# First attention of a two-layer decoder: where the maxima of the next heads stand, how the causal mask reaches them, and how the sums are grouped

## The chip, the cores and the metric

The kernel runs on one core of a Trainium2 chip. A core has TensorE (PE: matmuls, with PEld its weight loads), VectorE (DVE), ScalarE (ACT), GpSimd (POOL) and SyncE (SP, which here issues the DMAs). Each engine works through its own queue in order; semaphores make one wait for another. Matrix products land in PSUM, which has 8 banks of 128 partitions x 512 float32. The metric is the device time of one execution in microseconds, the median of the runs shown.

## What is computed

x is (4, 1024, 256) float32. Two layers follow each other, each with an attention, a cross attention to a context of 77 rows, and a feed-forward part:

```python
x = x + _L0_attn_ref(_layernorm(x), L0_attn_w_attn, L0_attn_w_proj)
x = x + _L0_xattn_ref(_layernorm(x), ctx_768, ...)
x = x + _L0_ffn_ref(_layernorm(x), ...)
x = x + _L1_attn_ref(_layernorm(x), L1_attn_W)
x = x + _L1_xattn_ref(_layernorm(x), ctx_768, ...)
x = x + _L1_ffn_ref(_layernorm(x), ...)
```

The change touches the first line alone, a causal attention of 16 heads of 16 columns with a bias that falls linearly with distance:

```python
q, k, v = jnp.split(x @ w_attn.T, 3, axis=-1)      # then (B, 16, 1024, 16)
att = jnp.einsum('bhqd,bhkd->bhqk', q, k) * (1.0 / math.sqrt(D))
rel = pos[None, :] - pos[:, None]
bias = jnp.where(rel <= 0, slopes * rel, -jnp.inf)
att = jax.nn.softmax(att + bias[None], axis=-1)
y = jnp.einsum('bhqk,bhkd->bhqd', att, v)
return y.transpose(0, 2, 1, 3).reshape(B, T, C) @ w_proj.T
```

## The kernel before

The first attention (A0) goes batch by batch, and in a batch by four groups of four heads. Queries and keys stand in two bfloat16 stacks per group, QS and KS, in which each value is split into several bfloat16 rows so that one matmul gives a nearly exact product; 12 further rows carry the bias, and two more rows of QS, against ones in KS, carry minus the row's maximum. So the maxima must be known before the scores are made.

**Maxima** (`a0_max`, L339). For a group, 38 units in all. Each unit fills a PSUM bank M with up to 512 columns of scores, query-major (L352), and DVE takes the maximum along the row (L357) into a small tile mt. There are 22 units whose last 128 columns lie on the diagonal: per half of the queries one with four heads side by side, two with two heads, and eight with one head and 384 or 512 columns. On these a further matmul adds the mask (L356: identity times a tile with -30000 above the diagonal). Sixteen units per group have no diagonal. Two PSUM banks serve M in turn. After each half, `a0_put_max` (L375) negates the maxima (L380), transposes them on PE (L381), splits them into two bfloat16 rows (L383, L384) and sends these by two small DMAs (L386) into rows 108 and 109 of QS.

**Units** (`a0_main`, L388). A unit is a chunk c of 256 queries and a block j of 128 keys up to the diagonal, 2 + 4 + 6 + 8 = 20 units per group. `scores` makes, key-major, S for two heads at a time in one of two banks (L401), adds the transposed mask on diagonal blocks (L403), and ACT takes the exponential into the tile P (L404), which has four buffers. `pv` makes the **sums** (L413): for each of the four heads V's 17 columns (16 of values, one of ones), padded to 32, times P, in float32, which PE runs as two passes. The four heads stand in four column tiles of 32, so eight instructions of PE make the sums of one unit. A unit's sums are issued two units later (`LAG0` = 2): whenever more than two are pending, the oldest is done. The list of pending ones is kept from one group to the next. When a chunk pair is through, `o_out` (L424) moves O out, transposes it (L430) and divides by the sum column.

**Order.** `A0` (L470) weaves a group's 20 units with the front work of the next group: its stacks (seven DMAs or so) and its 38 maxima. In the third group the first 12 steps of the next batch's front (layernorm, q, k and v) are woven in too, and in the fourth group the rest of that front, 44 steps with the first group's maxima of the next batch. `weave(a, na, b, nb)` takes the next step of whichever is behind in proportion, so that na steps of a go with nb steps of b; what is left of the one runs alone when the other is through. The weights of b are the row `NW`, 20 being that of a. Around all this a second weave adds the cross attention and feed-forward of the preceding batch, or, in the first batch, the preparation of weights. The program's order is not yet that of the queues: the build asks the framework to order every engine's queue by a simulated timeline (`schedule_with_timeline_sim=True`), so an instruction can come before others that stand ahead of it in the program, as far as data and buffers allow.

The second attention (A1, L923 to L927 for its sums) has the same form of sums, with 8, 16 or more instructions in a row. Its tile DL0 is allocated once, when it starts.

## Time and profile before

| what | value |
|---|---|
| median of 3 runs | 2410.97 us (2407.53 to 2416.93) |
| profiled execution | 2408.58 us |
| its span | 2406.8 us |
| PE busy | 2141.5 us, 89% |
| DVE busy | 1692.2 us, 70% |
| ACT busy | 1639.2 us, 68% |
| POOL busy | 1198.2 us, 50% |
| mean granted PE clock | 0.957 |
| maxima on DVE, L357 | 608 instructions, 386.2 us, mean 655 ns |
| maxima on PE, L352 | 768 instructions, 225.8 us busy |
| scores, L401 | 1280 instructions, 230.4 us busy |
| sums, L413 | 2560 instructions, 240.1 us busy |
| exponentials, L404 | 640 instructions, 342.4 us, mean 563 ns |

The span runs from the first to the last instruction of the program; the profiled execution's own time lies 1.8 us above it. Busy time counts an instant once even where several instructions of an engine overlap, as matmuls do: a matmul's duration runs from its start to the end of its way through the array, and the next one starts long before. So the distance from one start to the next says what a matmul costs in a full queue.

In the lists that follow, a waits row names the waiting engine and line, then who released it, the sum of the waiting in us, how often, and the longest. A row of the timeline gives start, duration, engine and line, and tiles, with equal neighbours merged (x2), and in brackets the idle time ahead of it with its releaser. A row by shape gives the count, busy us and mean ns, then the engine's idle time ahead and who ended it. A windows row gives, for a stretch of the span, each engine's busy time and count of instructions.

### The profile page before, as it was taken

What the parts mean: (1) busy time and instruction counts of PE and PEld (TensorE: products, weight loads), DVE (VectorE), ACT (ScalarE), POOL (GpSimd) and SP (SyncE); (2) the same over time, 40 slices, a digit from 0 to 9 for tenths busy, and PEclk for the clock granted to TensorE, in tenths of its full rate; (3) what the DMA queues carried; (4) which work ended last, traced back from release to release, by engine and by line L of the source; (5) the groups of instructions that cost most, each with busy time, mean ns of one, the idle gap of its engine ahead of it and who ended that gap; (6) DMA issues with size and microseconds to landing.
All of it is one profiled execution on the core that took longest, in us unless ns stands there. A gap on an engine that the chain in (4) does not pass through costs nothing.

```text
span 2406.8 us, 51445 instructions
## 1 busy us (share of the span) xinstructions
PE 2141.5 (89%) x19110; PEld 1510.9 (63%) x19110; DVE 1692.2 (70%) x3781; ACT 1639.2 (68%) x4173; POOL 1198.2 (50%) x1942
## 2 busy tenths in 40 slices
PE   6798899998999998899988988889988998899876
PEld 4454457755666654576656766567766766676675
DVE  4666657677766786776775677777867787777766
ACT  4365446676766676565778878987678777888542
POOL 7121313154331352412545458766867788775664
PEclk9899999999999999899989999999989999999988
DMA  8667331223841236231262224512241223542000
GB/s 260 199 193 211 116 90 44 66 61 108 242 135 44 64 111 188 69 73 41 81 185 53 71 71 129 149 38 56 98 111 43 56 74 119 105 98 71 10 10 18
DMA packets 182697, 238.45 MB, mean 99 GB/s; under 512 B 16198, under 2 KB 165846, under 8 KB 175958
## 3 DMA queue, kind: packets, MB, share of 16 engines
q1 hardware_dynamic: 182446, 235.15, 34.8%
q8 instruction: 151, 2.47, 0.4%
q14 instruction: 100, 0.82, 0.1%
HBM read 152.62 MB, written 82.21 MB: 98 GB/s over the span
## 4 chain that ended last, share of the span: by engine, by line
PE 59%; DVE 14%; DMA 8%; POOL 7%; ACT 7%; issue 3%; SPq 1%; POOLq 0%; DVEq 0%; ACTq 0%
PE T L191 10%; PE W L191 8%; PE O L413 7%; PE O L927 5%; PE S L401 5%; PE Q L191 4%; PE M L352 4%; PE S L898 3%; DVE P L904 2%; DVE s_mt L357 2%; PE W L630 1%; PE T L723 1%; DMA wst<-in_L_xattn_Wq 1%; POOL P L909 1%; ACT P L906 1%
## 5 line engine op out<-in xcount | busy, mean ns | idle before, releaser
L357 DVE TENSOR_REDUCE s_mt<-M 128x1 f32<-128x512 f32 (+3 forms) x608 | 386.2, 655 | 137.9 <-PE M L356 100.0
L404 ACT ACTIVATE P<-S 128x512 f32<-128x512 f32 (+1 forms) x640 | 342.4, 563 | 154.7 <-PE S L401 78.5
L906 ACT ACTIVATE P<-P,eps 128x1024 f32<-128x1024 f32 x320 | 344.5, 1082 | 57.2 <-DVE P L904 52.6
L904 DVE TENSOR_REDUCE P<-S 128x512 f32<-128x512 f32 (+1 forms) x480 | 284.8, 610 | 75.4 <-PE S L898 60.7
L352 PE MATMUL M<-KS,QS 108*128 108x512 bf16 (+3 forms) x768 | 225.8, 341 | 48.2 <-DVE s_mt L357 23.9
L191 PE MATMUL T<-R,xX 128*128 128x352 f32 (+1 forms) x1136 | 246.7, 331 | 4.8 <-ACT E L619 1.4
L898 PE MATMUL S<-QS,KS 96*128 96x256 bf16 (+1 forms) x1280 | 217.9, 269 | 36.9 <-DVE P L904 34.5
L401 PE MATMUL S<-QS,KS 110*128 110x256 bf16 (+1 forms) x1280 | 230.4, 267 | 16.9 <-ACT P L404 13.7
L413 PE MATMUL O<-P,V 128*32 128x256 f32 (+1 forms) x2560 | 240.1, 377 | 0.8 <-ACT P L404 0.6
L622 POOL TENSOR_TENSOR E<-E,s_xsm 128x616 f32<-128x616 f32 x64 | 77.9, 1217 | 323.7 <-DVE s_xsm L620 261.3
L191 PEld LDWEIGHTS T<-R,xX 128*128 128x128 f32 x1136 | 183.0, 190 | 24.7 <-ACT E L619 5.4
L191 PE MATMUL W<-R,xph 128*128 128x256 f32 (+1 forms) x952 | 185.4, 292 | 6.5 <-DVE xpl L180 4.8
L909 POOL TENSOR_TENSOR P<-P,y 128x512 f32<-128x512 f32 x128 | 165.1, 1299 | 34.0 <-ACT y L871 17.4
L619 ACT ACTIVATE E<-T,s_xmx 128x77 f32<-128x77 f32 x512 | 159.6, 334 | 28.6 <-DVE s_xmx L616 26.5
L401 PEld LDWEIGHTS <-KS 110*128 110x128 bf16 x1280 | 107.2, 100 | 105.6 <-issue 60.3
L927 PE MATMUL O<-P,VsJ 128*32 128x128 f32 x3584 | 168.2, 282 | 5.3 <-ACT P L906 4.8
L898 PEld LDWEIGHTS <-KS 96*128 96x128 bf16 x1280 | 101.8, 99 | 110.2 <-issue 88.9
L191 PEld LDWEIGHTS W<-R,xph 128*128 128x128 f32 (+1 forms) x952 | 149.5, 192 | 17.8 <-DVE xpl L180 6.9
L352 PEld LDWEIGHTS <-QS 108*128 108x128 bf16 x768 | 68.3, 100 | 128.0 <-issue 100.4
L191 PE MATMUL W<-R,xpl 128*128 128x256 f32 (+2 forms) x476 | 139.6, 293 | 1.0 <-DVE xpl L180 1.0
L730 POOL TENSOR_TENSOR R<-wst 128x256 f32<-128x256 f32 x128 | 92.3, 732 | 88.0 <-DVE wst L729 82.8
L179 ACT ACTIVATE xph<-W 128x512 fp32r<-128x512 f32 (+2 forms) x180 | 79.3, 458 | 80.1 <-PE W L633 32.8
(351 smaller groups left out, 5660.0 us busy)
## 6 DMA issues: line engine op xcount, KB each, us to landing
QS<-dr SPq DMA_DIRECT2D x144, 192.0 KB
KS<-dr SPq DMA_DIRECT2D x72, 384.0 KB
dr<-qp SPq DMA_DIRECT2D x32, 768.0 KB
MD<-R SPq DMA_DIRECT2D x24, 616.0 KB
UD<-R SPq DMA_DIRECT2D x24, 512.0 KB
R<-MD SPq DMA_DIRECT2D x32, 308.0 KB
X<-in_x SPq DMA_DIRECT2D x16, 512.0 KB
dr<-qp SPq DMA_DIRECT2D x32, 256.0 KB
```

The lines of the kernel that those rows point to most:

```text
L191: nc.tensor.matmul(out, x, y, start=first and n == 0, stop=last and n == len(seq) - 1)
L352: nc.tensor.matmul(Sv[:, x, 0:w], QS[:108, i // 4, hh, i % 4 * 128 : i % 4 * 128 + 128], KS[:108, hh, k0:k1], start=x == 0, stop=not diag ...
L357: nc.vector.tensor_reduce(out, Sv[:, :, 0:w], AX.X, ALU.max)
L401: nc.tensor.matmul(S[:, e, 0:w], st[1][:110, hh, j * 128 : (j + 1) * 128], st[0][:110, q0 // 512, hh, q0 % 512 : q0 % 512 + w], start=e == ...
L404: nc.scalar.activation(P[:, 2 * p : 2 * p + 2, 256 - w :], S[:, :, 0:w], AF.Exp)
L413: nc.tensor.matmul(O[0][hh * 32 : hh * 32 + 32, o + o0 : o + 256], V[j // 4][:, j % 4, h * 17 : h * 17 + 32], P[:, hh, o0:], start=c % 2 = ...
L619: nc.scalar.activation(E[:, n * 77 : (n + 1) * 77], Sv[:, k, :], AF.Exp, bias=mx[:, n : n + 1], accum_out=sm[:, n : n + 1])
L898: nc.tensor.matmul(S[:, e, 0:w], st[r][1][:96, hh, j * 128 : (j + 1) * 128], st[r][0][:96, q0 // 512, hh, q0 % 512 : q0 % 512 + w], start= ...
L904: nc.vector.tensor_reduce(Pv, S[:, :, 0:w].unsqueeze(3), AX.X, ALU.max, apply_absolute_value=True)
L906: nc.scalar.activation(Pw, Pw, AF.Square, bias=self.eps1)
L909: nc.gpsimd.tensor_tensor(Pd, Pd, Ds[r, c][:, j - 2 * c], ALU.mult)
L927: nc.tensor.matmul(Oc[rows, o0 : o0 + 128], lhs, P[:, hh, c0 : c0 + 128], start=j == 2 * c and i == 2 * c, stop=fin and i == 2 * c + 1)
```

## The change

Three edits to the first attention.

1. The weave weights of the front work go from 25, 25, 38, 38 per 20 units to 42, 42, 54, 48.
2. On diagonals of one head, the mask matmul goes. DVE adds a mask tile of 512 columns (zeros, and the triangle in its last 128; the last w columns of it are used) and takes the maximum in one `tensor_tensor_reduce`, which also writes the masked scores back to PSUM. The tile `mask4` is loaded at the start, in the buffer of the tag DL0. Diagonals of two and four heads stay as they are.
3. Sums wait until three units are pending, and then two units' sums are issued together (`LAG0` = 1, `PAIR` = 2). `issue_after` puts what they issue on PE behind the present unit's last score or mask matmul, in the order of the queue and without a wait for its end.

```diff
+    c["mask4"] = np.concatenate([np.zeros((128, 384)), c["maskb"].astype(np.float32)], 1).astype(bf)
...
-    LAG0, LAG1 = 2, 2
+    LAG0, LAG1, PAIR = 1, 2, 2
     GQ, NQ = (2, 2, 2, 2), (12, 12, 12, 12)
-    NW = ((25, 25, 38, 38),) * 4
+    NW = ((42, 42, 54, 48),) * 4
...
         self.const(("identb", BF), ("maskb", BF), ("maskTb", BF))
+        self.mask4 = self.t([128, 512], BF, "DL0")
+        self.nc.sync.dma_start(self.mask4, self.c["mask4"])
...
-                nc.tensor.matmul(Sv[:, x, 0:w], QS[:108, i // 4, hh, i % 4 * 128 : i % 4 * 128 + 128], KS[:108, hh, k0:k1], start=x == 0, stop=not diag and x == n - 1)
-            if diag:
-                r = self.maskb if n == 1 else self.maskb.unsqueeze(1).to_broadcast([128, n, 128])
-                o = Sv[:, 0, w - 128 : w] if n == 1 else Sv[:, :, w - 128 : w]
-                nc.tensor.matmul(o, self.identb, r, start=False, stop=True)
-            nc.vector.tensor_reduce(out, Sv[:, :, 0:w], AX.X, ALU.max)
+                nc.tensor.matmul(Sv[:, x, 0:w], QS[:108, i // 4, hh, i % 4 * 128 : i % 4 * 128 + 128], KS[:108, hh, k0:k1], start=x == 0, stop=(n == 1 or not diag) and x == n - 1)
+            if diag and n > 1:
+                nc.tensor.matmul(Sv[:, :, w - 128 : w], self.identb, self.maskb.unsqueeze(1).to_broadcast([128, n, 128]), start=False, stop=True)
+            if diag and n == 1:
+                nc.vector.tensor_tensor_reduce(S[:, 0:w], S[:, 0:w], self.mask4[:, 512 - w :], 1.0, -3e38, ALU.add, ALU.max, out)
+            else:
+                nc.vector.tensor_reduce(out, Sv[:, :, 0:w], AX.X, ALU.max)
...
-                    nc.tensor.matmul(S[:, e, 0:w], st[1][:110, hh, j * 128 : (j + 1) * 128], st[0][:110, q0 // 512, hh, q0 % 512 : q0 % 512 + w], start=e == 0, stop=not dg and e == 1)
+                    self.lead = nc.tensor.matmul(S[:, e, 0:w], st[1][:110, hh, j * 128 : (j + 1) * 128], st[0][:110, q0 // 512, hh, q0 % 512 : q0 % 512 + w], start=e == 0, stop=not dg and e == 1)
                 if dg:
-                    nc.tensor.matmul(S[:, :, 0:128], self.identb, self.maskTb.unsqueeze(1).to_broadcast([128, 2, 128]), start=False, stop=True)
+                    self.lead = nc.tensor.matmul(S[:, :, 0:128], self.identb, self.maskTb.unsqueeze(1).to_broadcast([128, 2, 128]), start=False, stop=True)
...
-            if len(pend) > self.LAG0:
-                f, a = pend.popleft()
-                f(*a)
+            if len(pend) >= self.LAG0 + self.PAIR:
+                with self.tc.issue_after(self.lead.ins):
+                    for _ in range(self.PAIR):
+                        f, a = pend.popleft()
+                        f(*a)
             yield
```

## The prediction

> **What bounds the kernel now.** I read the windows first, to see which engine fills the first attention, then the waits, then the order of time on TensorE (PE), then the rows by shape. The first attention's score units (L401) run from 99 to 1274 us; I cut that stretch at the four batches:

> ```profile
> core 0: us, PE busy (x) PEld busy (x) DVE busy (x) ACT busy (x) POOL busy (x), PEclk, DMA share, GB/s
> 100.00:350.00 250.00, 220.20 (x1781) 125.44 (x1780) 154.20 (x290) 139.43 (x291) 54.21 (x55) 0.93 0.57 162
> 350.00:665.00 315.00, 296.89 (x2415) 199.78 (x2413) 223.59 (x504) 214.38 (x628) 110.67 (x156) 0.99 0.36 101
> 665.00:975.00 310.00, 291.83 (x2306) 187.76 (x2304) 226.04 (x518) 201.01 (x597) 99.69 (x148) 0.97 0.39 110
> 975.00:1285.00 310.00, 286.07 (x2240) 192.72 (x2241) 214.67 (x496) 203.99 (x618) 111.42 (x175) 0.94 0.32 88
> ```

> PE is busy 88% in the first batch and 92 to 94% in the other three (1095 of 1185 us together); VectorE (DVE) has 818.5 us (69%), ScalarE (ACT) 758.8 (64%). So time taken from PE's queue here is time taken from the span, and DVE and ACT have room. The waits say where PE loses time:

> ```profile
> PEld O L413 <- issue: 79.6, 377, 0.4
> PE M L352 <- DVE s_mt L357: 23.9, 49, 2.0
> PE S L401 <- ACT P L404: 13.7, 16, 3.6
> ```

> The first is not a wait for data. 377 times the weight load of the sums (L413, P times V in 32-column tiles) is held for some 0.2 us: the price of going over to 32 columns, once per block of sums. There are 16 groups x 20 units = 320 units, so the scheduler cuts 57 of them in two. The second is a maximum that finds both its PSUM banks still unread by DVE. In order of time, one block each of PE's kinds:

> ```profile
> 317.11 0.32 PE L352 MATMUL M<-KS,QS 108*128 108x384 bf16 x1
> 317.27 0.22 PE L356 MATMUL M<-maskb,identb 128*128 128x128 bf16 x1
> 317.33 0.38 PE L401 MATMUL S<-QS,KS 110*128 110x256 bf16 x2
> 317.64 0.64 PE L413 MATMUL O<-P,V 128*32 128x256 f32 x8
> 318.21 0.34 PE L352 MATMUL M<-KS,QS 108*128 108x384 bf16 x1
> ...
> 463.53 0.38 PE L401 MATMUL S<-QS,KS 110*128 110x256 bf16 x2
> 463.75 0.60 PE L630 MATMUL W<-ident,E 128*128 128x128 f32 x4
> ```

> What an instruction costs in a full queue is the distance to the next start, not its duration: the mask matmul (L356) takes 317.33 - 317.27 = 0.06 us, a unit of sums 318.21 - 317.64 = 0.57. Two score matmuls take 0.22 when an untiled matmul follows (463.53 to 463.75), 0.31 when sums follow (317.33 to 317.64): **entering costs 0.09 us**.

> What leaving costs is read where tiled blocks of two lengths occur, in the second attention:

> ```profile
> 1305.82 0.64 PE L927 MATMUL O<-P,VsJ 128*32 128x128 f32 x16
> 1306.40 0.28 PE L898 MATMUL S<-QS,KS 96*128 96x128 bf16 x2
> ...
> 1314.62 0.43 PE L927 MATMUL O<-P,V 128*32 128x128 f32 x8
> 1314.98 0.41 PE L191 MATMUL T<-R,xX 128*128 128x308 f32 x1
> ```

> Eight instructions of 128 columns take 0.36 us to the next start, sixteen 0.58. Eight more cost 0.22, so the first eight hold 0.36 - 0.22 = 0.14 us that is paid once: **leaving costs 0.14 us**, a block 0.23 in all beside its streaming.

> **The change part by part.** The profiled execution took 2408.6 us (span 2406.8 and 1.8 around it); the median of the runs is 2411.0, 2.4 above. I sum against 2408.6 and add 2.4 at the end.

> *Sums of two units together.* 320 units become 160 pairs. If the scheduler cuts as often as now (57 times), 377 blocks become 217: 160 x 0.23 = 36.8 us less on PE. Bounds: no cuts, 217 x 0.23 = 49.9; every pair cut apart, 57 x 0.23 = 13.1 at most, or nothing. I take 36.8, since cuts come from other work that gets ready during a block, and the time in blocks hardly changes. The edge that puts the sums behind the unit's last score matmul is an order, not a wait. Behind that matmul stand the pair, the next maxima and the other layers' matmuls; the matmul itself waits for its PSUM bank, freed by the preceding unit's exponentials (L404). These are just what the younger sums of the pair need, so the pair finds its P ready. The lag of one adds no wait there, but it takes the sums away from between two units' scores: that is the rival below. Four P buffers hold the pair, the unit at hand and one more.

> [...]

> *Mask and maximum in one step.* Of a group's 38 maxima 16 are one-head diagonals, so 256 mask matmuls go (the row below counts them): 256 x 0.06 = 15.4 us less on PE. Their weight loads go too; they lay beside matmuls. For it DVE's reduction becomes one with two inputs that also writes PSUM.

> ```profile
> L356 PE MATMUL M<-maskb,identb 128*128 128x128 bf16 x256 | 57.3, 224 | 0.0
> L357 DVE TENSOR_REDUCE s_mt<-M 128x1 f32<-128x512 f32 x384 | 254.5, 683 | 61.9 <-PE M L352 34.9 <-PE M L356 25.1
> L180 DVE TENSOR_TENSOR xpl<-W,xph 128x512 fp32r<-128x512 f32 x90 | 61.0, 678 | 11.0 <-ACT xph L179 10.6
> ```

> The trace has no such operation. Lower end: it costs what the reduction costs, since a two-input pass with one input in PSUM takes 678 ns against 683, so 0; a gain is excluded by that. Upper end: a pass and a reduction one after the other, 0.68 us more, 174 us of DVE. I take 0, by the nearest row (one pass, two inputs); DVE's 366 idle us of this stretch cover it. With the cover gone, in the lone maxima of 71 to 98 us (DVE busy 24.1 of 27), all 16 of the first group would show: 11 us at the upper end.

> [...]

> *Maxima beside the units.* A group has 20 units and 38 maxima, beside which batches put further front work in the third and fourth groups (50 and 44 steps). At 25, 25, 38, 38 steps per 20 units, 13, 13, 12 and 6 steps are left when the units are through; at 42, 42, 54, 48 none. The leftovers are visible: from 293.7 to 301.0 twelve maxima run alone, each so:

> ```profile
> 294.31 0.38 PE L352 MATMUL M<-KS,QS 108*128 108x512 bf16 x1 [0.22 <-DVE s_mt L357]
> ```

> 0.60 us from start to start, DVE's pace, with 0.22 of PE idle. Of the 23.9 us of such waits I put 10 to such stretches (in most others the other layers fill PE) and count **10 us** gained; bounds 0 and 20. With a maximum go its reduction and, per half group, the steps of the put (L372, L380, L381, L383, L384) and two one-row DMAs. On SP these are issued earlier against the next half's q and k stores and ahead of the next group's stacks; POOL's queue holds none of it. They land while the last two units run; today scores wait for them after 301.0, until 308.8. Per unit there are now 1.9 maxima: 1.3 us of DVE beside some 1.6 of PE (scores 0.44, sums 0.57, maxima with masks 0.5 to 0.6), so PE stays the longer.

> *The mask tile.* One DMA of 128 KB, some 0.45 us on SP ahead of the first x load. It takes the buffer DL0, whose second-attention load (192 KB) is now issued at 14.6 us and must go behind the last maximum, and the second attention starts only after its gates (L788, 1233 us; last maximum 1215). In and out about cancel: 0.

> **Sum.** PE loses 36.8 + 15.4 = 52.2 us. Three batches turn it all into time; the first, at 88% PE and with DMA busy 0.57, half of its quarter: 52.2 x 0.875 = 45.7. Maxima 10. Against it: score matmuls waiting for exponentials, 13.7 us now, may as much as double with no sums between two units: 10 us. 2408.6 - 45.7 - 10 + 10 = 2362.9, and 2.4: **2365 us**. Its own range: all cuts gone and all of it turned into time with 14 us of maxima and no new waits, 2411 - 49.9 - 15.4 - 14 = 2332; pairs half as good and the maxima worth nothing, 2411 - 15.4 - 18 + 10 = 2388.

> **Rivals.**

> *The pairs don't hold, or PE isn't what sets the pace.* If the scheduler puts other matmuls into the pairs, or DMA and the other layers' chains set the pace, the masks' 15.4 us remain: 2411 - 15 = **2396**. For it: 57 of 320 units are cut already, and an order behind the scores says nothing about what comes between. Against: PE at 92 to 94%.

> *The new DVE step is two passes.* DVE 818 + 174 = 992 us, 84% of the stretch; 11 us in the lone maxima, and waits for maxima (23.9) doubled: 2365 + 11 + 24 = **2400**. For it: no row of such an operation. Against: the two-input row's 678 ns.

> *Scores wait for exponentials: slower.* In each pair the second unit's scores come with no sums before them. Its two PSUM banks are freed by the first unit's two exponentials, 0.61 us each (L404, 512 wide), 1.21 together; between stand only scores and some two maxima, about 0.94 us. If ACT is at another layer's work (64% busy), another half us: 160 x 0.5 = 80 us, 2365 + 80 = **2445**. It decides from 45 / 160 = 0.28 us per pair on. For it: PE's queue is in order, so the sums that filled this place can't. Against: in three batches the other layers' matmuls stand ready to fill it, and there are only 16 such waits now.

> **How the numbers follow.** Forecast 0.62; first rival 0.17, two passes 0.08, slower 0.13. What a measurement of this kernel can tell from no change is about 0.5%, 12 us: faster is below 2399. Faster: 0.62, most of the first rival (0.10) and a little of the two passes (0.03), 0.75; same 0.12; slower 0.13. The range takes in the forecast's own and both rivals near 2400: 2332 to 2402. The forecast's own alone is 2332 to 2388.

> **What would show it.** Right: some 217 entries into the sums and rows of x16; 96 mask matmuls; the new DVE row near 0.68 and 0.55 us; no stretch of a dozen maxima without scores; the last score unit some 45 us earlier, and the second attention as long as before. Wrong: entries still above 300; a DVE row above 1 us; waits of L401 for L404 of 50 us or more, which would bring the slower case.

## The result, and the profile after

The changed kernel takes **2435.51 us** (median of 4 runs, 2431.08 to 2438.18), the kernel before 2412.89 beside it on the same chip (2407.53 to 2416.93): a ratio of 1.0097, 95% interval 1.0069 to 1.0125. It is 1% slower; 2365 was forecast, with a range up to 2402. The profiled execution took 2437.2 us, its span 2435.4, and the mean granted PE clock is 0.942, against 0.957.

The windows of the changed kernel, cut at its four batches as before (per stretch: length, busy time and instructions of each engine, granted clock, DMA share, GB/s):

```profile
core 0: us, PE busy (x) PEld busy (x) DVE busy (x) ACT busy (x) POOL busy (x), PEclk, DMA share, GB/s
100.00:350.00 250.00, 213.92 (x1718) 121.98 (x1717) 163.57 (x357) 138.24 (x291) 54.08 (x56) 0.92 0.58 163
350.00:672.00 322.00, 295.07 (x2331) 197.95 (x2340) 226.14 (x565) 212.29 (x624) 107.93 (x154) 0.97 0.35 98
672.00:987.00 315.00, 282.02 (x2236) 185.59 (x2246) 225.68 (x578) 199.94 (x600) 99.45 (x147) 0.94 0.39 106
987.00:1298.00 311.00, 279.91 (x2202) 190.89 (x2211) 218.36 (x551) 205.12 (x621) 112.33 (x176) 0.91 0.33 92
```

PE has less to do in all four stretches together (1070.9 us where it had 1095.0), and yet they are longer (1198 against 1185 us). In the last two PE is busy 90%, no longer 92 to 94. The granted clock is lower in each of the four.

The waits of PE in the changed kernel (engine and line, releaser, us in all, times, longest):

```profile
PEld O L417 <- issue: 73.7, 328, 0.4
PE M L355 <- DVE s_mt L361: 24.7, 41, 5.7
PE M L355 <- DVE s_mt L359: 9.9, 16, 2.6
PE M L355 <- DMA KS<-c_alk: 24.1, 5, 7.6
PE S L405 <- ACT P L408: 16.1, 22, 2.5
```

Entries into the sums fell from 377 to 328, not to 217. Waits of the maxima for DVE rose from 23.9 us (49 times) to 34.6 (57), 9.9 of it behind the new step (L359): half as much again, not the double of the second rival. Waits for the DMA of the key stack rose from 5.4 to 24.1 us, and scores wait for exponentials 16.1 us instead of 13.7: the slower rival, which needed 45, did not come.

The new DVE step, in the rows by shape (output and input, count, busy us and mean ns, idle ahead):

```profile
L359 DVE CUSTOM_DVE_ANT_0 M<-M,DL 128x512 f32<-128x512 f32 x128 | 88.6, 703 | 20.3 <-PE M L355 19.9
L359 DVE CUSTOM_DVE_ANT_0 M<-M,DL 128x384 f32<-128x384 f32 x128 | 71.1, 564 | 22.8 <-PE M L355 22.2
L359 DVE DVE_READ_ACCUMULATOR2_ANT s_mt<- 128x1 f32 x256 | 36.1, 141 | 0.0
```

It is one pass, 703 ns for 512 columns against 681 of a reduction, and a second instruction of 141 ns reads the accumulator.

And the stretch in which twelve maxima ran alone before the change is still there, in order of time on PE:

```profile
294.67 0.38 PE L355 MATMUL M<-KS,QS 108*128 108x512 bf16 x1 [0.22 <-DVE qr L292]
295.27 0.38 PE L355 MATMUL M<-KS,QS 108*128 108x512 bf16 x1 [0.22 <-DVE s_mt L361]
295.87 4.59 PE L355 MATMUL M<-KS,QS 108*128 108x512 bf16 x7 [0.22 <-DVE s_mt L361]
301.24 0.58 PE L355 MATMUL M<-KS,QS 108*128 108x512 bf16 x1 [0.78 <-DVE s_mt L361]
```

Counted over the first attention, stretches of six or more maxima without a score between them, each from its first maximum's start to its last one's end: 10 with 123 maxima and 102 us before, 10 with 112 maxima and 104 us after. So the first edit does not do what it says: the weave gives the program's order, and the order of the queues comes from the framework's timeline.

### Where the time went

```profile
302.25 0.63 PE L191 MATMUL Q<-yTh,WAl 128*128 128x512 f32 x1
302.68 0.63 PE L191 MATMUL Q<-yTh,WAh 128*128 128x512 f32 x1
...
306.97 0.39 PE L191 MATMUL Q<-yTh,WAl 128*128 128x512 f32 x1
307.20 0.39 PE L191 MATMUL Q<-yTh,WAh 128*128 128x512 f32 x1
```

The same matmul takes 0.43 us from start to start before 305.0 and 0.23 after it; the clock record is half from 298.2 to 305.0.

So a stretch of the span divides into three sums without remainder: **work** (PE's busy time, the part at half clock counted half), **clock** (the other half of it) and **idle**. The span is cut where the second attention's first score matmul starts, 1274.4 us before and 1287.5 after:

```profile
core 0: us, PE busy (x) PEld busy (x) DVE busy (x) ACT busy (x) POOL busy (x), PEclk, DMA share, GB/s
100.00:1274.40 1174.40, 1086.41 (x8669) 698.77 (x8668) 811.80 (x1790) 750.26 (x2109) 375.71 (x530) 0.96 0.40 113
1274.40:2406.80 1132.40, 990.00 (x10111) 764.83 (x10107) 824.20 (x1869) 851.70 (x1991) 770.21 (x1319) 0.96 0.27 73
```

and the changed kernel:

```profile
100.00:1287.50 1187.50, 1062.43 (x8418) 689.61 (x8445) 827.04 (x2034) 747.10 (x2110) 373.50 (x531) 0.94 0.40 112
1287.50:2435.40 1147.90, 1010.70 (x10102) 777.41 (x10107) 827.69 (x1869) 851.62 (x1991) 771.45 (x1319) 0.95 0.27 72
```

Length less PE busy is the idle time, 88.0 and 125.1 us in the first attention. With the busy time that lies in half-clock stretches (first attention 76.3 and 110.3, second part 72.9 and 99.5):

| us | first attention: work | clock | idle | second part: work | clock | idle |
|---|---|---|---|---|---|---|
| before | 1048.2 | 38.2 | 88.0 | 953.6 | 36.4 | 142.4 |
| after | 1007.2 | 55.2 | 125.1 | 961.0 | 49.8 | 137.2 |
| difference | -41.0 | +17.0 | +37.1 | +7.4 | +13.3 | -5.2 |

-41.0 + 17.0 + 37.1 = +13.1 and +15.5 make the 28.6 us of the two spans. PE's work did shrink, by 41 us of the 52 forecast; all of it and more came back as idle time and as half clock. The second part executes the same instructions in both kernels, only in another order. Its work term shows what this division is good for: over all 18 kernels of this study it lies between 948 and 964.

Each such division is of one execution. The 61 executions of the kernel before that ran beside the experiments took 2402.83 to 2421.59 us (median 2412.19), at granted clocks of 0.948 to 0.959, the longer ones mostly at the lower clock (correlation -0.67). The profiled one, 2408.58 us at 0.957, would be the fourteenth shortest of them, and one alone has a higher clock. So a few us between two profiles say little, and part of any loss against this profile is its own good luck.

### The profile page after: what moved, and what is told of

Read it like the earlier page. It is cut to its first block, busy times and chain, and to the rows that moved or that the text cites. A ratio compares the mean times of both kernels' runs of the same rounds, so it can differ in the third digit from the quotient of the medians.

```text
span 2435.4 us, 51121 instructions
## 1 busy us (share of the span) xinstructions
PE 2138.1 (88%) x18818; PEld 1512.1 (62%) x18854; DVE 1708.7 (70%) x4037; ACT 1634.2 (67%) x4173; POOL 1196.8 (49%) x1942
## 4 chain that ended last, share of the span: by engine, by line
PE 55%; DVE 14%; ACT 9%; DMA 8%; POOL 8%; issue 4%; SPq 1%; POOLq 0%; ACTq 0%; DVEq 0%
PE T L192 9%; PE W L192 8%; PE O L417 6%; PE O L933 5%; PE Q L192 5%; PE S L405 4%; PE M L355 4%; PE S L904 3%; DVE P L910 2%; DMA KS<-c_alk 2%; DVE s_mt L361 1%; PE W L636 1%; ACT P L912 1%; ACT V L625 1%; POOL P L915 1%
## 5 line engine op out<-in xcount | busy, mean ns | idle before, releaser
L361 DVE TENSOR_REDUCE s_mt<-M 128x1 f32<-128x512 f32 (+2 forms) x352 | 235.3, 682 | 90.7 <-PE M L357 48.5
L904 PE MATMUL S<-QS,KS 96*128 96x256 bf16 (+1 forms) x1280 | 219.0, 269 | 37.4 <-DVE P L910 31.4
L405 PE MATMUL S<-QS,KS 110*128 110x256 bf16 (+1 forms) x1280 | 232.9, 270 | 21.1 <-ACT P L408 16.1
L417 PE MATMUL O<-P,V 128*32 128x256 f32 (+1 forms) x2560 | 211.7, 380 | 0.1
L192 PEld LDWEIGHTS T<-R,xX 128*128 128x128 f32 x1136 | 187.0, 193 | 25.7 <-issue 6.4
L359 DVE CUSTOM_DVE_ANT_0 M<-M,DL 128x384 f32<-128x384 f32 (+1 forms) x256 | 158.3, 633 | 43.1 <-PE M L355 42.1
L933 PE MATMUL O<-P,VsJ 128*32 128x128 f32 x3584 | 175.2, 285 | 7.0 <-ACT P L912 6.6
L192 PEld LDWEIGHTS W<-R,xph 128*128 128x128 f32 (+1 forms) x952 | 152.8, 195 | 13.3 <-DVE xpl L181 5.7
```

Of the source, the lines that this page charges most:

```text
L192: nc.tensor.matmul(out, x, y, start=first and n == 0, stop=last and n == len(seq) - 1)
L361: nc.vector.tensor_reduce(out, Sv[:, :, 0:w], AX.X, ALU.max)
L405: self.lead = nc.tensor.matmul(S[:, e, 0:w], st[1][:110, hh, j * 128 : (j + 1) * 128], st[0][:110, q0 // 512, hh, q0 % 512 : q0 % 512 + w] ...
L417: nc.tensor.matmul(O[0][hh * 32 : hh * 32 + 32, o + o0 : o + 256], V[j // 4][:, j % 4, h * 17 : h * 17 + 32], P[:, hh, o0:], start=c % 2 = ...
L904: nc.tensor.matmul(S[:, e, 0:w], st[r][1][:96, hh, j * 128 : (j + 1) * 128], st[r][0][:96, q0 // 512, hh, q0 % 512 : q0 % 512 + w], start= ...
L933: nc.tensor.matmul(Oc[rows, o0 : o0 + 128], lhs, P[:, hh, c0 : c0 + 128], start=j == 2 * c and i == 2 * c, stop=fin and i == 2 * c + 1)
```

## The experiments

Each expectation names the theories that it weighs. The runs of one series were on one chip. Unless said otherwise each kernel is the kernel before with the edit shown, and the ratio is to the kernel before in the same series.

### Each part by itself

Weights alone:

```diff
-    NW = ((25, 25, 38, 38),) * 4
+    NW = ((42, 42, 54, 48),) * 4
```

> The weave weights of the change alone. Theory W (the weights are to blame: maxima asked for earlier make TensorE's in-order queue wait for the next group's stacks and for DVE): 15 to 30 us slower than before, waits of the maxima's matmuls for DMA near 24 us as in the changed kernel (16 before). Theory of the DVE step and theory of the pairs: within 8 us of before. Theory C (reordering and clock: every edit reshuffles all queues, and the granted clock falls with each extra gap): anything within 20 us, with the second attention's length moving as well although nothing in it is changed.

The DVE step alone, with its mask tile:

```diff
+            if diag and n == 1:
+                nc.vector.tensor_tensor_reduce(S[:, 0:w], S[:, 0:w], self.mask4[:, 512 - w :], 1.0, -3e38, ALU.add, ALU.max, out)
```

> The mask and maximum in one DVE step alone (mask tile in DL0). Theory D (the step is to blame: 0.14 us of accumulator read behind each, banks held longer): 10 to 25 us slower than before. Theories of the weights and of the pairs: 5 to 15 us faster, by the 15.4 us of mask matmuls that are gone. Theory C: anything within 20 us, the second attention moving too.

The pairs alone:

```diff
-    LAG0, LAG1 = 2, 2
+    LAG0, LAG1, PAIR = 1, 2, 2
...
+            if len(pend) >= self.LAG0 + self.PAIR:
+                with self.tc.issue_after(self.lead.ins):
```

> Sums of two units together, alone. Theory P (the pairs are to blame: sums no longer fill the place between two units' scores): 10 to 25 us slower, waits of scores for exponentials well above 14 us. Theories of the weights and of the DVE step: 5 to 20 us faster, since entries into the sums fall from 377 to about 330 at 0.23 us. Theory C: anything within 20 us.

Weights of 27 instead of 25, a change of two steps in 25 for the first two groups:

```diff
+    NW = ((27, 27, 38, 38),) * 4
```

> A control that is next to nothing: weave weights 27 in place of 25 in the first two groups of each batch, all else as before. Theories of the weights, of the DVE step and of the pairs: within 4 us of before. Theory C: up to 15 us away either way, with another order in all queues and another length of the second attention.

Measured: weights 1.0091 (1.0068 to 1.0115), DVE step 1.0014 (0.9997 to 1.0032), pairs 1.0006 (0.9987 to 1.0026), weights of 27 1.0085 (1.0055 to 1.0116). **The whole loss goes with the weights**, and two steps of weight cost nearly as much as the full edit. Neither other part is worth anything by itself: both miss the 10 to 25 us of loss of the theories against them and the gains of the others. The weights cost by another way than their theory said: the waits for the key stack, put near 24 us, are 9.7 in e1.

### The two other parts together, and more weights

Step and pairs, without the weights:

```diff
-    LAG0, LAG1 = 2, 2
+    LAG0, LAG1, PAIR = 1, 2, 2
     NW = ((25, 25, 38, 38),) * 4
...
+            if diag and n == 1:
+                nc.vector.tensor_tensor_reduce(S[:, 0:w], S[:, 0:w], self.mask4[:, 512 - w :], 1.0, -3e38, ALU.add, ALU.max, out)
```

> The changed kernel with the old weave weights: DVE step and pairs together. If the parts add (the step +0.14%, the pairs +0.06%, the weights +0.91% alone, the whole change +0.97%): within 10 us of before, and 20 us faster than the changed kernel. If the step and the pairs are worth their PE time (15 and 11 us, not seen when each was made alone because of the clock): 15 to 30 us faster than before.

Weights of 23, 18 and 26 on the kernel before:

```diff
+    NW = ((23, 23, 38, 38),) * 4
...
+    NW = ((18, 18, 38, 38),) * 4
...
+    NW = ((26, 26, 38, 38),) * 4
```

> Weights 23 in place of 25 in the first two groups, else before. Theory W (more maxima beside the units is worse, step by step): 2 to 20 us faster than before, as 27 was 20 slower. Theory L (25 is a lucky order, and any other order is worse, the loss being in the granted clock and in the second attention too): 8 to 25 us slower, like 27.

> Weights 18: half of the maxima run alone behind the units. Theory W: clearly faster than before or, if lone maxima do cost what their waits show, up to 10 us slower. Theory L: 8 to 30 us slower.

> Weights 26. Theory W: 5 to 12 us slower, between 25 and 27. Theory L: 0 to 25 us slower, in no order with 23 and 27; its second attention another one again.

Measured: step and pairs 0.9921 (0.9894 to 0.9947), weights of 23 1.0094 (1.0062 to 1.0125), of 18 1.0081 (1.0051 to 1.0111), of 26 1.0061 (1.0041 to 1.0082). **Edits 2 and 3 together gain 0.8%** (medians 2394.99 and, of the kernel before beside it, 2409.82 us, 0.6%). The windows of that kernel, cut in the same way:

```profile
100.00:1261.90 1161.90, 1049.66 (x8415) 686.74 (x8438) 816.91 (x2033) 747.67 (x2110) 375.41 (x530) 0.95 0.41 114
1261.90:2394.80 1132.90, 997.53 (x10100) 768.23 (x10107) 826.31 (x1869) 852.47 (x1991) 770.48 (x1319) 0.96 0.28 73
```

The second part is as long as before (1132.9 against 1132.4), and the first attention is 12.5 us shorter, with 36.8 us less of PE's busy time and 24.2 more of idle time.

Of the weights, each of the three loses, to either side of 25, by one step as well as by seven. So it does not follow the number of maxima beside the units, and the profiles show where it happens (length of the first attention from 100 us on, and of the second part):

| kernel | first attention: length | work | clock | idle | second part: length | clock |
|---|---|---|---|---|---|---|
| before (25) | 1174.4 | 1048.2 | 38.2 | 88.0 | 1132.4 | 36.4 |
| e7, 18 | 1165.6 | 1041.6 | 34.9 | 89.0 | 1152.9 | 49.2 |
| e6, 23 | 1173.9 | 1048.5 | 37.4 | 88.0 | 1152.4 | 55.4 |
| e8, 26 | 1176.0 | 1050.1 | 37.1 | 88.8 | 1143.7 | 46.9 |
| e4, 27 | 1182.0 | 1050.1 | 37.2 | 94.8 | 1150.7 | 52.8 |
| e1, 42, 42, 54, 48 | 1194.5 | 1051.1 | 45.2 | 98.2 | 1144.5 | 51.1 |
| e2, step | 1176.1 | 1040.5 | 38.4 | 97.3 | 1143.3 | 47.5 |
| e3, pairs | 1189.2 | 1026.1 | 54.5 | 108.6 | 1120.2 | 30.0 |
| e5, step and pairs | 1161.9 | 1005.3 | 44.3 | 112.2 | 1132.9 | 38.0 |

With 18, 23 and 26 the first attention is as long as before or shorter, and the loss of 11 to 21 us stands in the second part, whose code is not touched. The profiled executions of 18 and 23 lie 10.6 and 7.4 us below their kernels' medians, so this shows where part of the loss is, not all of it. The windows of weights of 23:

```profile
100.00:1273.90 1173.90, 1085.94 (x8640) 698.07 (x8664) 809.00 (x1789) 750.35 (x2107) 375.68 (x530) 0.96 0.40 113
1273.90:2426.30 1152.40, 1011.60 (x10103) 779.04 (x10112) 828.87 (x1871) 855.40 (x1992) 769.85 (x1319) 0.94 0.27 71
```

Beside the kernel before: 0.5 us less in the first, 20.0 more in the second, at clock 0.94 instead of 0.96. Weights of 27 and of 23 have the same order of matmuls on PE in the second part, and there they take 1150.7 and 1152.4 us. Weights of 42 (e10, below) and of 60 share one order too, and take 1144.9 and 1147.6 there. All other kernels have an order of their own in the second part: it is drawn anew with nearly every edit of the first, and an order goes with a length. Of the 18 kernels the second part of the kernel before is the third shortest (1120 to 1153, mean of the other 17: 1142.5). A line through the 18 gives 1084 us + 0.48 per us of half-clock time (idle time in it included), with 4 us left over (9.7 at weights of 18): what differs is mostly the time at half clock. That this time is a cause there rests on the matmuls' visible distances and on this line; no run held the clock up by other means, and filling PE's holes was not tried.

The pairs show the other thing. Alone they take 22.1 us of work from PE, and 20.6 of idle time and 16.3 of clock come in its place; the shortest second part of all hides that in the total.

### A kernel that beats both

Step and pairs with weights of 18, the shortest first attention of the series before:

```diff
     LAG0, LAG1, PAIR = 1, 2, 2
+    NW = ((18, 18, 38, 38),) * 4
```

> DVE step and pairs with weights 18 in the first two groups. If the first attention gets shorter with fewer maxima beside its units (it ended at 1265.6 us with 18, 1273.9 with 23, 1282 with 27, 1294.5 with the change's weights): its first part ends near 1253, 9 us before that of the version with 25. If the second attention's length is drawn by the order of the queues: anything from 1120 to 1153 for it, so 2375 to 2410 in all, and its length 1081 plus half of its time at half clock, within 6 us.

Weights for the first two groups alone, and for the last two alone:

```diff
+    NW = ((42, 42, 38, 38),) * 4
...
+    NW = ((25, 25, 54, 48),) * 4
```

> The change's weights in the first two groups of a batch only (42, 42, 38, 38), all else before. If these are what costs: the first part ends 10 to 20 us later than before's 1274; if the third and fourth groups cost it, within 6 us of it. Second part between 1120 and 1153 by its order.

> The change's weights in the last two groups only (25, 25, 54, 48). The counterpart of the run before: the first part 10 to 20 us later than 1274 if these groups cost it, else within 6 us. Second part between 1120 and 1153.

A barrier of all engines between the two attentions of the kernel before, to part the second's order from the first's:

```diff
+    K.tc.strict_bb_all_engine_barrier()
     K.phase = 1
```

> The kernel before with a barrier of all engines ahead of the second attention, nothing else changed. If the order of the queues decides the second attention's time: its first part stays at 1274 within 5 us, its second part becomes another draw between 1120 and 1155 (before's own is 1132), at 1081 plus half of its time at half clock, some us more for the barrier. If the second attention's time is set by what the first leaves behind (transfers under way, engines out of step): it is that of before within 3 us beside the barrier's few.

Measured: **step and pairs with 18: 0.9892 (0.9868 to 0.9916), 2387.14 us, the shortest of the study**; first two groups 1.0118 (1.0098 to 1.0138); last two 1.0011 (0.9997 to 1.0025); barrier 1.0059 (1.0034 to 1.0084). The windows of the first of these:

```profile
100.00:1252.20 1152.20, 1046.22 (x8446) 680.07 (x8445) 813.67 (x2037) 750.82 (x2110) 375.59 (x532) 0.96 0.41 115
1252.20:2387.80 1135.60, 996.19 (x10111) 766.04 (x10107) 825.51 (x1869) 850.79 (x1992) 769.87 (x1319) 0.95 0.28 73
```

Here 40.6 us of work are gone, idle time has grown by 18.0 and clock by 0.5 us: 22.2 us are kept in the first attention. This is the weave turned the other way, with more maxima left alone (129 in 11 stretches). Its interval overlaps that of step and pairs at 25, so which of these two weights is better is not settled. By the times of the whole kernel the loss by weights comes from the first two groups alone. The division is less clear: with the last two groups' weights the first attention took 1184.4 us, 10.0 more, which was the sign set for a cost of these groups; 11.3 of it is work, clock and idle are 1.3 less. The barrier says little: the second part took 1139.1 us, in another order than before, and the first 9.3 more, where it was to stay within 5, so neither theory is decided.

### The size of the weight in the first attention

Two further weights on the kernel before, and two on step and pairs:

```diff
+    NW = ((34, 34, 38, 38),) * 4
...
+    NW = ((60, 60, 38, 38),) * 4
...
     LAG0, LAG1, PAIR = 1, 2, 2
+    NW = ((10, 10, 38, 38),) * 4
...
     LAG0, LAG1, PAIR = 1, 2, 2
+    NW = ((34, 34, 38, 38),) * 4
```

> Weights 34 in the first two groups, else before. By size: the first part ends between 1282 and 1292 us. By luck of the order: anywhere from 1265 to 1292. The second part 1081 plus half of its time at half clock, within 8 us.

> Weights 60 in the first two groups, else before. By size: the first part ends at 1292 us or later. By luck: anywhere from 1265 to 1292. The long stretches of maxima without scores are still there, as with 42 (13 of them against 10 before).

> Step and pairs with weights 10 in the first two groups. By size: the first part ends at 1252 us or earlier. By luck: anywhere from 1245 to 1285. More lone maxima than with 18 (129), with no loss from them.

> Step and pairs with weights 34 in the first two groups. By size: the first part ends between that of 25 (1262) and that of the whole change (1287), near 1272. By luck: anywhere from 1245 to 1290.

Measured: 34 gives 1.0152 (1.0104 to 1.0200), 60 1.0127 (1.0058 to 1.0196); on step and pairs 10 gives 0.9960 (0.9947 to 0.9974) and 34 1.0070 (1.0037 to 1.0102). In the first attention:

| weight of the first two groups | 18 | 23 | 25 | 26 | 27 | 34 | 42 (e10) | 60 |
|---|---|---|---|---|---|---|---|---|
| length | 1165.6 | 1173.9 | 1174.4 | 1176.0 | 1182.0 | 1197.6 | 1192.2 | 1195.1 |
| of it clock and idle | 123.9 | 125.4 | 126.2 | 125.9 | 132.0 | 149.2 | 144.5 | 146.0 |
| us of lone maxima | 133 | 116 | 102 | 102 | 115 | 137 | 137 | 137 |

Above 27 the first attention is some 20 us longer and stays so; the work is unchanged, all of it is idle time and clock.

But these are not three readings of a size. The profiles of 42 and 60 list the same instructions in the same order on PE, DVE, ACT and POOL, and 34 has 8 of this part's 9003 matmuls elsewhere: one order, three times, and a longer one. For 34 both theories had put the end of this part at 1292 us at most; it came at 1297.6. Weights of 23 and 27 also share an order, but for 35 of 8972 matmuls, and take 1173.9 and 1182.0 us. On step and pairs the lengths are 1162.9 (10), 1152.2 (18), 1161.9 (25) and 1174.6 (34): the least stands at 18. By size, 10 was to end at 1252 us or earlier, with more lone maxima than the 129 of 18; it ended at 1262.9 with 125, in an execution of 2408.44 us where the median is 2400.10. So a weight works by the order that comes of it, and not step by step. From 25 up the length goes with the lone maxima, which become more, not fewer; from 18 to 25 it does not, nor on step and pairs, where 18 has 125 us of them and is the shortest.

By batches, each to its last score, the 17.8 us of the first two groups' weights are +0.4, +3.1, +8.6 and +5.7; in the profile of 60, of the same order, +1.9, +3.3, +12.0 and +3.6. Why the framework's order leaves more holes with them stays open.

## Why the prediction was wrong

**What bounds the kernel.** Right as far as it went: PE's queue. But PE has two more accounts, holes and the half clock they bring, and the prediction read both in its windows (PEclk 0.93 and 0.94 in the first and last batch, 90 of 1185 us idle) and put new holes at no more than 10 us of waits for exponentials, and the clock at nothing.

**The step that failed first: "Three batches turn it all into time".** Work fell by 41.0 us in the changed kernel and by 42.9 with step and pairs alone, so a fifth of the 52.2 was missing. Of the 42.9, 24.2 came back as idle time and 6.1 as clock: 12.5 us were kept, where 45.7 were counted. By what ended it, the idle time grew by 9.3 us behind ACT, 5.3 behind DVE, 3.7 behind POOL, 3.2 behind DMAs and 2.8 in gaps of under 0.15 us; in the changed kernel by 16.7 behind DVE, 8.2 behind ACT and 7.9 behind DMAs. That is no single chain. That all of them had been nearly as long as PE's queue, at 92 to 94%, and a shorter queue met them sooner, is how this reads; no run tested it.

**The pairs.** Near in size, by luck. Forecast were 217 entries and 36.8 us; 328 came, 49 x 0.23 = 11.3 us at the forecast's price. But the price was wrong as well: a cut costs more than an entry, since half a unit takes as long as a whole one. In the kernel before, in order of time:

```profile
310.32 0.63 PE L413 MATMUL O<-P,V 128*32 128x256 f32 x4
310.88 0.39 PE L191 MATMUL Q<-WAh,yTh 128*128 128x256 f32 x1
```

Four instructions take 0.56 us to the next start, and eight took 0.57 (317.64 to 318.21): a unit cut in two pays 0.56 and an entry twice. All sums, each block from its start to the next start, waits left out and half clock counted half, took 207.86 us before, 185.03 with the pairs alone, 177.40 with step and pairs and 182.13 in the changed kernel. So of the 36.8 us 25.7 came there, beside up to 0.09 for each of 67 blocks fewer.

In PE's order by the records there were 395 blocks of sums before, 148 of them less than a unit; after it 328, 60 of them less than a unit, 242 just one and only 26 more than one. So the edit mended units that were cut, and hardly made pairs: "the scheduler cuts as often as now" was wrong, since the edge holds the sums behind a score matmul and nothing holds two units' sums together. Pairs that can't be cut were not tried.

The condition of the rival that gave 2396 was met, and step and pairs without the weights measured 2394.99; that is luck, for the rival had the masks' 15.4 us turn into time, and not 42.9 us of work of which 12.5 stay. Where a pair did hold, its weight loads took no time of their own, as two rows of the kernel before let one expect: eight sums of 256 columns took 0.57 us to the next start (317.64), sixteen of 128, with twice the loads, 0.58 (1305.82). In the changed kernel, in order of time:

```profile
459.56 0.38 PE L405 MATMUL S<-QS,KS 110*128 110x256 bf16 x2
459.88 1.07 PE L417 MATMUL O<-P,V 128*32 128x256 f32 x16
460.88 0.39 PE L355 MATMUL M<-KS,QS 108*128 108x512 bf16 x1
...
1081.08 0.64 PE L417 MATMUL O<-P,V 128*32 128x256 f32 x8
1081.65 0.39 PE L405 MATMUL S<-QS,KS 110*128 110x256 bf16 x2
```

Sixteen took 1.00 us to the next start and eight 0.57: eight more cost 0.43, which is 0.57 less the 0.14 of leaving.

**Mask and maximum in one step.** 96 mask matmuls were left and the row is near the bound that was taken (703 ns where the two-input row had 678); the 36.1 us of accumulator reads beside it lie inside the bounds of 0 to 174 us of DVE. Of the 41.0 us of work that are gone in the changed kernel, 25.7 are sums and 15.3 the rest, where 15.4 were counted for the masks. By itself the step took 7.7 us of work from PE: its order cut more units (404 blocks, 167 less than a unit), and the sums took 5.7 us more. In total it gave nothing.

**Maxima beside the units: -10.** Wrong in its condition: the lone stretches remained. Wrong in sign: the weights cost 18 to 20 us in the first attention alone, and 25.6 on top of step and pairs (1161.9 to 1187.5, 12.9 of it idle and 10.9 clock). This is the dearest step: from step and pairs to the whole change the span grows by 40.6 us, 25.6 here and 15.0 in the second part, where it is a matter of the order drawn.

**Scores waiting for exponentials: +10.** 2.4 us came. The forecast time of that rival, 2445, lies near the result, by a mechanism that did not occur.

**"The second attention as long as before".** Wrong, +15.5 us, 13.3 of it clock. Together: 41.0 - 37.1 - 17.0 - 15.5 = 28.6 us lost, where 45.7 were to be won. Part of the 15.5 may be the scatter of single executions.

**The mask tile.** 0 was about right: the first score came at 101.6 us instead of 99.5, and between 99.0 and 105.3 in kernels without the tile.

## What to carry to other kernels

A busy share of 92% does not mean that work taken from an engine is time gained (here 42.9 us of work gave 12.5): ask which chain stands right behind it, and price the hole. Where a framework makes the queues' order, nearly any edit draws it again, here with 10 us of mean loss in code that was not touched (some of it the good execution that was profiled): test the parts one by one, and each at several harmless settings, before a gain or loss is put down to the idea. The good part of this change was found by leaving out the part that lost.

## What the runs showed of the hardware

**The half clock follows PE's idle time by a grid.** Half-clock stretches begin on a grid of 3.413 us. Over the 18 profiled executions, windows of this grid by PE's busy share in them, and how many of the next windows were at half speed:

| busy share of the window | under 0.4 | 0.4 to 0.5 | 0.5 to 0.6 | 0.6 to 0.7 | 0.7 to 0.9 | over 0.9 |
|---|---|---|---|---|---|---|
| at full speed: next at half | 258 of 258 | 163 of 182 | 150 of 272 | 72 of 460 | 6 of 1907 | 0 of 8051 |
| at half speed: next at half | 149 of 149 | 61 of 61 | 52 of 52 | 95 of 95 | 229 of 264 | 42 of 656 |

A window less than half busy is followed by one at half speed (421 of 440), and from there mostly a window that is nearly full brings full speed back (614 of 656, against 35 of 264 at 0.7 to 0.9). No long gap led to the drop at 298.2 us in the kernel before: in the window ahead of it none was over 0.22 us. It held lone maxima, 0.60 us apart with 0.38 busy, a share of 0.63 (of windows at 0.6 to 0.7, 72 of 460 were followed by half speed). So a stretch that ran at DVE's pace cost its holes, 0.22 us in each 0.60, and then nearly double time in the matmuls behind it, 0.43 us instead of 0.23.

**The step with an accumulator is two DVE instructions.** Each of the 256 such steps of the changed kernel is a pass (703 ns at 512 columns, 564 at 384) and a read of the accumulator, which took 141 ns, 256 times, with no idle time ahead of it.

**Four column tiles cost little more than one.** Blocks of 2, 4, 6 and 8 sums of 256 columns, over the kernel before at full clock, take 0.55, 0.56, 0.565 and 0.57 us to the next start (medians of 23, 80, 15 and 185 blocks): the four heads' sums run beside each other (in the block at 317.64 us four instructions start within 0.02 us, the other four 0.24 us after the first), and a block's time goes by its units, full or cut, 0.57 us for one and 1.00 for two.
